# Gated cross-attention and mixture of experts on one core: memory rows picked before the branch, tokens in two buffers, later weights on ScalarE's queue, last lists after the first expert tiles

## The chip, the core and the metric

The kernel runs on one core of a Trainium2 chip. The core has TensorE for matrix products, VectorE, ScalarE and GpSimd for the rest, SyncE for issuing transfers, and 16 DMA engines that all queues share. Each engine works through its own list of instructions in order; semaphores tie the lists together. The metric is device time in microseconds (us). The kernel before takes 276.34 us, the median of 3 runs (274.91 to 276.58).

## What is computed

There are 8 sequences of 256 tokens with 512 features, and for each sequence a memory of 256 rows, of which a mask allows a part. All is float32.

```
x = x + tanh(g_x) * attention(layernorm(x), memory, mask)    # scores / sqrt(512), masked softmax, readout
y = layernorm(x)
p = softmax(y @ w_router.T)                 # 8 experts, the best 2 of each token, weights renormalised
x = x + tanh(g_f) * sum over the 2 experts of weight * (silu(y @ gate.T) * (y @ up.T)) @ down.T    # 192 inner features
```

2048 tokens with 2 experts each make 4096 pairs of a token and an expert.

## The kernel before

**Memories.** The mask leaves at most 64 rows of each memory with this data, so two memories share a tile of 128 rows, and there are four such pairs. `m_find` counts along the mask; for a pair, `m_hot` (L221) makes a matrix that marks which row goes to which place, `m_pick` (L228) multiplies it with the row numbers on TensorE, and `m_fetch` (L234) adds an offset on VectorE and has GpSimd gather the rows. Pair 0 is fetched at once. Then comes a branch (L745): the long arm treats memories with more than 64 rows and isn't taken; the short one starts the loads of the remaining tokens (L751 to 753). Pairs 1 to 3 are picked and fetched inside the loop that follows. `m_mean`, `m_centre`, `m_turn` and `m_route` centre a pair's rows, transpose them, and project them on the router. Three products on zeros (L742) stand before the branch on TensorE.

**Attention.** A written-out loop (L759) runs over 16 token tiles of 128, with the stages of different tiles interleaved: step `s` holds `a_probs` (transpose of the probabilities) and `a_values` of tile s-1, `a_scores` of tile s, `a_stats` (mean and variance on VectorE) of tile s+3, and `a_scale` (inverse deviation, GpSimd) of a later pair of tiles. The order in this loop is the order on each engine. `a_values` also yields the router's logits and the best two experts of each token.

**Lists.** Tokens are sorted into lists, one per expert, by pairs of tiles. `f_mark` counts, `f_rank` (L459) turns counts into places with three small products and VectorE, and builds two matrices of zeros and ones, `at_row` and `at_col`; four of the `at_col` products run mostly on GpSimd (L485). `f_table` (L488) adds them into one table in TensorE's accumulator. `f_weigh` (L431) computes weights on ScalarE and stores the pair's tokens with their logits as rows of `xc_d` in device memory. `read_table` turns the table into token numbers. The first tile of each expert's list uses only the first ten token tiles, so it can be gathered early; the rest needs the whole table.

**Experts.** There are 36 tiles of 128 listed tokens: 8 first tiles, 24 more, and 4 whose expert is read at run time. `gather` (L626) has GpSimd fetch a tile's rows from `xc_d` into a ring of 12 slots, which lies over the token buffer `xall`. `step(s)` (L709) does `fetch` (up to 6 tiles ahead), `gate_up` of tile s, `flip` of s-1, `turn` (transposes) of s+2 and `down` of s-2; the result is added into the output by an indirect accumulating transfer from GpSimd (L683). Steps 0 to 4 are interleaved with the end of the lists (L818 to 832): step 0 stands before the last table, steps 1 to 4 among reading it.

**Weights.** Each expert has a gate-and-up half of 768 KB and a down half of 384 KB. SyncE issues those of experts 0 to 3 in loop steps 2 to 9 and all eight halves of experts 4 to 7 at once in step 16.

Of the kernel before, what the change touches and what calls it, by code (L numbers as in the profile page):

```python
# [48 lines left out]
def gated_xattn_moe(ctx: ExitStack, tc: tile.TileContext, x, xT, ctxn, ctxT, mask, maskT, g_x, g_f, wr, wgu, wd, out):  # L49
# [62 lines left out]
    nc.sync.dma_start(out=mk8, in_=maskT)  # L112
    xall = xp.tile([P, NT, D], FP, name="xall")
    xs = [xall[:, i, :] for i in range(NT)]
    xTs = []

    def load_x(lo, hi):
        nc.sync.dma_start(out=xall[:, lo:hi, :], in_=x[lo * P:hi * P, :].rearrange("(i p) d -> p i d", p=P))

# [19 lines left out]
    def load_half(n):  # L139
        e, part = divmod(n, 2)  # L140
        if part == 0:
            nc.sync.dma_start(out=wgu_sb[:, e * GU:(e + 1) * GU], in_=wgu[:, e * GU:(e + 1) * GU])
        else:
            nc.sync.dma_start(out=wd_sb[:, e * DN:(e + 1) * DN], in_=wd[:, e * DN:(e + 1) * DN])

# [82 lines left out]
    def m_pick(p):  # L228
        n, oh = P if p else 1, KEEP.pop(("oh", p))
        for c in range(MC):  # L230
            nc.tensor.matmul(pidx[:, p:p + n], lhsT=oh[:, c].rearrange("p h v -> p (h v)"), rhs=mval[:, c, 0:n],
                             start=(c == 0), stop=(c == MC - 1))
# [63 lines left out]
    def m_hide(b):  # L296
        nc.gpsimd.tensor_scalar(hide[:, b, :], slot, cnt[:, b:b + 1], BIG, ALU.is_ge, ALU.mult)

    def long_way():
# [6 lines left out]
        mv, rs, vg, nmx, den, ng = (one[k] for k in ("l_mv", "l_rs", "l_vg", "l_nmx", "l_den", "l_ng"))  # L306
        load_x(TT, NT)
        for b in range(B):
# [43 lines left out]
    def a_stats(i):  # L352
        if i % 2 == 0:
            KEEP["mv", i // 2] = sm_.tile([P, 2, 2], FP, tag="mvp", bufs=3, name=f"mvp_{i}")
        st = sm_.tile([P, 6], FP, tag="st", name=f"st_{i}")
        nc.vector.bn_stats(st, xs[i])
        nc.vector.bn_aggr(KEEP["mv", i // 2][:, i % 2, :], st)
# [101 lines left out]
    def f_rank(k):  # L459
# [22 lines left out]
        for n in range(4):  # L482
            i = 2 * k + n // 2
            by = nc.vector if k >= NT // 2 - 2 and n < 2 else nc.gpsimd
            by.tensor_scalar(at_col[:, n, :], cols_w if by is nc.vector else cols, low[:, n:n + 1], idt[:, i, n % 2:n % 2 + 1], ALU.is_equal, ALU.mult)  # L485
# [129 lines left out]
    def x_store(k):  # L615

        nc.sync.dma_start(out=out[2 * k * P:2 * (k + 1) * P, :].rearrange("(i p) d -> p i d", p=P), in_=xall[:, 2 * k:2 * k + 2, :])

# [4 lines left out]

    KEEP["ring"], RING = 0, 12

    def gather(q):  # L626

        k = RING if apart else KEEP["ring"]
        g = xall.rearrange("p i d -> p (i d)")[:, k * XW:(k + 1) * XW]
        if not apart:  # L630
            KEEP["ring"] = (k + 1) % RING
        src = xc_d[0:EARLY * P, :] if q < E else xc_d[:, :]
        nc.gpsimd.indirect_dma_start(out=g, out_offset=None, in_=src,  # L633
                                     in_offset=bass.IndirectOffsetOnAxis(ap=gids[:, q:q + 1], axis=0))
        KEEP["xg", q] = g
# [62 lines left out]
    def at(f, s):  # L698
        if 0 <= s < len(order):
            f(order[s])  # L700

    KEEP["next"], KEEP["known"] = 0, E - 2

    def fetch(upto):
        while KEEP["next"] <= min(upto, KEEP["known"]):
            gather(order[KEEP["next"]])
            KEEP["next"] += 1

    def step(s):  # L709
        fetch(s + AHEAD)  # L710
        at(gate_up, s)
        at(flip, s - 1)
        at(turn, s + 2)
        at(down, s - 2)
# [11 lines left out]
    with tc.manual_schedule(engines={PE, DVE, ACT, POOL, SP}):  # L726
# [8 lines left out]
        a_stats(0)  # L735
        a_stats(1)
        a_scale(0)
        r_centre()
        m_hide(0)
        idle = bank([P, D], "idle")  # L740
        for n in range(3):
            nc.tensor.matmul(idle, lhsT=ones, rhs=busy, start=True, stop=True)  # L742
# [16 lines left out]
        for s in range(NT + 2):  # L759
            odd = s % 2  # L760
            p, part = divmod(s, 4)
            on(a_probs, s - 1)
            if s == EARLY + 2:
                f_close()
            on(f_centre, s - 2)
            if s:
                on(a_stats, s + 3)
                if not odd:
                    on(a_scale, (s + 2) // 2, NT // 2)
            if s != 1:  # L770
                on(a_scores, s)
            if s == 0:
                m_hot(1)
                m_hot(2)
                for b in range(1, B):
                    m_hide(b)
                more_constants()
                a_scores(1)
                m_route(0)
                m_pick(1)  # L780
                a_stats(2)
                m_fetch(1)
                a_stats(3)
                a_scale(1)
            if 1 <= s < NP - 1:
                m_pick(s + 1)
                m_fetch(s + 1)
                if s + 2 < NP:
                    m_hot(s + 2)
            if part == (2 if p else 3) and p + 1 < NP:  # L790
                m_centre(p + 1)
            on(f_square, s - 2)
            if odd:
                on(f_rank, (s - 3) // 2, NT // 2)
            if s == EARLY + 3:
                read_table(pick[:, 0:E], 0, E)
            on(a_values, s - 1)
            if s == NT:
                turn(order[0])
            if s == 1:  # L800
                nc.tensor.matmul(table, lhsT=ones[0:1, :], rhs=zero[:, 0:P], start=True, stop=True)
            if odd:
                on(f_weigh, (s - 5) // 2, NT // 2 - 1)
            else:
                on(f_scale, (s - 4) // 2, NT // 2 - 1)
                on(f_mark, (s - 2) // 2, NT // 2 - 1)
                on(f_table, (s - 4) // 2, NT // 2 - 1)
            if s == NT - 4:
# [9 lines left out]
            if s == NT + 1:  # L818
                turn(order[1])
                f_weigh(NT // 2 - 1)  # L820
                step(0)
                f_table(NT // 2 - 1)
                take_table("all")
                step(1)
                read_table(pick[:, E:NS], E, NS)
                KEEP["known"] = len(order) - 1
                step(2)
                f_total(NT // 2 - 1)
                step(3)
                numbers()  # L830
                step(4)
                read_table(sel, NS, NQ)
            if part == (1 if p else 2) and p + 1 < NP:
                m_mean(p + 1)
            if part == 3 and p + 1 < NP:
                m_turn(p + 1)
            if part == 0 and 0 < p < NP:
# [3 lines left out]
            if not odd and 3 <= (s + 4) // 2 < B:  # L841
                load_batch((s + 4) // 2)
            if 2 <= s < 2 + E:
                load_half(s - 2)
            if s == NT:
                for n in range(E, 2 * E):
                    load_half(n)
            if NT - 2 <= s <= NT:
                fetch(2 * (s - NT + 2) + 1)
        for n in range(5, len(order) + 2):  # L850
            step(n)
# [32 lines left out]
```

## Time and profile before

The profiled execution took 274.26 us.

| | |
|---|---|
| median of the runs | 276.34 us (274.91 to 276.58) |
| profiled execution | 274.26 us, its span 272.5 us |
| TensorE busy in the span | 242.0 us (89%) |
| GpSimd, VectorE, ScalarE busy | 155.7, 110.9, 109.7 us |
| gate and up products, all tiles | 99.2 us |
| down products, all tiles | 67.6 us |
| data moved | 48.20 MB, 177 GB/s on average |
| share of the 16 DMA engines by queue | 42.0% GpSimd's, 23.1% SyncE's, 4.6% ScalarE's |

In the profile PE is TensorE's products, PEld its loads of the stationary side, DVE VectorE, ACT ScalarE, POOL GpSimd and SP SyncE; L653 is line 653 of the kernel. A float32 product is recorded as two passes. A wait is put down to the event that came last in the profile. PEclk is the clock that the throttle granted, 1.00 being full speed; it shows a change only from its first event on.

### The profile page before, as it was taken

Reading aid. Unit: us, or ns where it says so; the run is one execution under the profiler, and the core shown is the slowest. Engines: PE = TensorE matmul, PEld = TensorE weight load, DVE = VectorE, ACT = ScalarE, POOL = GpSimd, SP = SyncE. Lnnn points to the kernel's source line nnn. Section 1 sums busy time; section 2 is a strip of 40 time slices with the busy share of each in tenths; the row PEclk is TensorE's granted clock in tenths of the full one; section 3 lists DMA queues with packets and bytes.
Section 4 is the critical chain, followed back from the end, with each engine's and each line's share of the span. In section 5 each row is a group of like instructions: output and inputs, shape, how many; then the busy total and the mean of one; then the engine's idle time right before and its main releaser. Section 6 shows DMA issues by size and latency. Waiting matters only on the chain.

```text
span 272.5 us, 3465 instructions
## 1 busy us (share of the span) xinstructions
PE 242.0 (89%) x1002; PEld 148.4 (54%) x1002; DVE 110.9 (41%) x447; ACT 109.7 (40%) x264; POOL 155.7 (57%) x249
## 2 busy tenths in 40 slices
PE   4788597878956999999999999999999999999950
PEld 4286374656633655556555555565555555655520
DVE  2357779897883434312312213123122131231310
ACT  1244467777775232333333323333333233333230
POOL 3898478789888006345536564584563657243360
PEclk9979899999999999999999999999999999999995
DMA  4599969999389997544565958485684595626374
GB/s 109 199 290 392 309 200 331 325 368 355 151 259 329 402 361 157 120 84 82 91 113 115 171 90 161 82 142 111 106 160 95 109 177 92 115 40 79 38 97 65
DMA packets 18684, 48.20 MB, mean 177 GB/s; under 512 B 2528, under 2 KB 2528, under 8 KB 18656
## 3 DMA queue, kind: packets, MB, share of 16 engines
q0 software_dynamic: 8416, 21.11, 42.0%
q1 hardware_dynamic: 8064, 22.04, 23.1%
q10 hardware_dynamic: 2176, 4.72, 4.6%
q8 instruction: 12, 0.20, 0.3%
q14 instruction: 16, 0.13, 0.2%
HBM read 29.51 MB, written 18.35 MB: 176 GB/s over the span
## 4 chain that ended last, share of the span: by engine, by line
PE 61%; POOL 3%; issue 2%; ACT 0%; POOLq 0%
PE pgu L653 32%; PE py L677 21%; PE pt_g L190 5%; PE pht L668 3%; POOL out L683 2%; POOL ac L485 1%; POOL spacer L503 0%; POOL xr L427 0%; ACT y L682 0%; POOLq L717 0%; PE pid L606 0%; PE table L492 0%; PE total L456 0%; POOLq L683 0%; PE total L455 0%
## 5 line engine op out<-in xcount | busy, mean ns | idle before, releaser
L653 PE MATMUL pgu<-wgu_sb,xT_g 128*128 128x384 f32 (+1 forms) x288 | 99.2, 487 | 0.0
L683 POOL DMA_INDIRECT out<-y,ids x36 | 57.1, 1586 | 69.3 <-DMA out<-y,ids 23.3
L653 PEld LDWEIGHTS pgu<-wgu_sb,xT_g 128*128 128x128 f32 x288 | 54.2, 190 | 44.4 <-issue 15.6
L677 PE MATMUL py<-wd_sb,hT 96*128 96x512 f32 (+1 forms) x144 | 67.6, 592 | 0.0
L659 DVE SCALAR_TENSOR_TENSOR th<-th,pgu 128x192 f32<-128x192 f32 x36 | 12.8, 354 | 123.4 <-ACT th L658 119.7
L633 POOL DMA_INDIRECT xall<-xc_d,gids x36 | 35.8, 995 | 23.6 <-DVE nti L589 13.6
L658 ACT ACTIVATE th<-pgu,xall 128x192 f32<-128x192 f32 x36 | 15.1, 420 | 68.0 <-PE pgu L653 63.7
L682 ACT ACTIVATE y<-py,w 128x512 f32<-128x512 f32 x36 | 24.7, 687 | 40.0 <-PE py L677 34.0
L677 PEld LDWEIGHTS py<-wd_sb,hT 96*128 96x128 f32 x144 | 24.5, 190 | 17.8 <-issue 17.5
L485 POOL TENSOR_SCALAR ac<-cols,low,idt 128x128 f16<-128x128 f32 x28 | 24.3, 877 | 8.1 <-DVE low L475 8.0
L192 ACT COPY xT_g<-pt_g 128x512 f32<-128x512 f32 x36 | 21.0, 584 | 9.8 <-PE pt_g L190 8.5
L372 PE MATMUL psc<-cT,xT 128*128 128x137 f32 x128 | 20.5, 310 | 2.8 <-ACT cT L284 2.1
L190 PE MATMUL pt_g<-ident,xall 128*128 128x128 f32 x144 | 21.6, 273 | 0.7 <-PE rank L463 0.7
L372 PEld LDWEIGHTS psc<-cT,xT 128*128 128x128 f32 x128 | 18.7, 217 | 4.4 <-ACT cT L284 3.0
L190 PEld LDWEIGHTS pt_g<-ident,xall 128*128 128x128 f32 x144 | 16.9, 140 | 1.7 <-PE rank L463 0.9
L402 PE MATMUL pav<-cn,prT 128*128 128x512 f32 x32 | 16.4, 594 | 0.0
L668 PEld LDWEIGHTS pht<-ident,h 128*96 128x96 f32 x72 | 9.1, 126 | 12.0 <-issue 7.2
L661 DVE SCALAR_TENSOR_TENSOR h<-th,xall,pgu 128x192 f32<-128x192 f32 x36 | 14.9, 415 | 1.3
L503 POOL MEMSET spacer<- 1x1 f32 x25 | 15.3, 612 | 0.0
L670 DVE COPY hT<-pht 96x256 f32<-96x256 f32 x36 | 14.9, 414 | 0.4 <-PE pht L668 0.4
L668 PE MATMUL pht<-ident,h 128*96 128x128 f32 x72 | 13.7, 273 | 0.0
L412 ACT ACTIVATE xr<-xall,xr 128x512 f32<-128x512 f32 x16 | 11.6, 723 | 2.0 <-DVE xall L408 1.9
(187 smaller groups left out, 243.1 us busy)
## 6 DMA issues: line engine op xcount, KB each, us to landing
wgu_sb<-wgu SPq DMA_DIRECT2D x8, 768.0 KB
xc_d<-xr ACTq DMA_DIRECT2D x8, 576.0 KB, 5.9
xT<-xT SPq DMA_DIRECT2D x8, 512.0 KB, 4.1
out<-xall SPq DMA_DIRECT2D x8, 512.0 KB
wd_sb<-wd SPq DMA_DIRECT2D x8, 384.0 KB, 9.0
xall<-x SPq DMA_DIRECT2D x1, 2048.0 KB
xall<-x SPq DMA_DIRECT2D x2, 512.0 KB
xall<-x SPq DMA_DIRECT2D x1, 1024.0 KB, 8.2
```

Source lines behind the costliest of these rows:

```text
L190: nc.tensor.transpose(pt[:, c, :], src[:, c * P:(c + 1) * P], ident)
L192: nc.scalar.copy(dst, pt)
L372: nc.tensor.matmul(both, lhsT=xTs[b][:, c, t * P:(t + 1) * P], rhs=cTs[p % 2][:, c, :], start=(c == 0), stop=(c == HC - 1))
L402: nc.tensor.matmul(pav, lhsT=prT, rhs=cns[p], start=True, stop=True)
L485: by.tensor_scalar(at_col[:, n, :], cols_w if by is nc.vector else cols, low[:, n:n + 1], idt[:, i, n % 2:n % 2 + 1], ALU.is_equal, ALU.mult)
L503: nc.gpsimd.memset(spacer, 0.0)
L633: nc.gpsimd.indirect_dma_start(out=g, out_offset=None, in_=src, in_offset=bass.IndirectOffsetOnAxis(ap=gids[:, q:q + 1], axis=0))
L653: nc.tensor.matmul(pgu, lhsT=xgT[:, c, :], rhs=span(wgu_sb, v * GU + c * 2 * I, 2 * I), start=(c == 0), stop=(c == HC - 1))
L668: nc.tensor.transpose(pht[:, k, :], h[:, k * IH:(k + 1) * IH], ident)
L677: nc.tensor.matmul(py, lhsT=hT[:, k, :], rhs=span(wd_sb, v * DN + k * D, D), start=(k == 0), stop=(k == 1))
L682: nc.scalar.activation(y, py, AF.Copy, scale=w)
L683: inst = nc.gpsimd.indirect_dma_start(out=out[:, :], out_offset=bass.IndirectOffsetOnAxis(ap=ids[:, q:q + 1], axis=0), in_=y, in_offset=No ...
```

## The change

- Pairs 1 to 3 of the memories are marked, picked and fetched before the branch, each with a product on one column of row numbers instead of 128. Two products on zeros stay there instead of three.
- The tokens lie in two buffers of 8 tiles; the gather ring has 14 slots, 7 over each.
- In the attention loop scores are issued for tile s+1 in step s, statistics for s+4; means, transposes and centring of the memories stand at other steps.
- Weights of experts 0 to 3 start in steps 4 to 7 and 10 to 13 on SyncE; those of experts 4 to 7 start on ScalarE's queue, one half in each of the expert steps 0 to 7.
- The first two `turn`s stand ahead of tile 15's values and logits or right behind them, the first gathers one loop step earlier. The table of pair 6 and the ranks of pair 7 stand behind step 0, the table of pair 7 behind step 1, and every later piece one step later, up to step 5. The weights of pairs 5 and 6 are made later. For the last two pairs all `at_col` products run on VectorE.

```diff
-    xall = xp.tile([P, NT, D], FP, name="xall")
-    xs = [xall[:, i, :] for i in range(NT)]
+    xhs = [xp.tile([P, NT // 2, D], FP, name=f"xh_{k}") for k in range(2)]
+    xs = [xhs[i // (NT // 2)][:, i % (NT // 2), :] for i in range(NT)]
...
     def load_half(n):
         e, part = divmod(n, 2)
+        by = nc.sync if n < E else nc.scalar
...
     def m_pick(p):
-        n, oh = P if p else 1, KEEP.pop(("oh", p))
+        n, oh = 1, KEEP.pop(("oh", p))
...
-            by = nc.vector if k >= NT // 2 - 2 and n < 2 else nc.gpsimd
+            by = nc.vector if k >= NT // 2 - 2 else nc.gpsimd
...
-    KEEP["ring"], RING = 0, 12
+    KEEP["ring"], RING = 0, 14
...
+    LOADS = (4, 5, 6, 7, 10, 11, 12, 13)
...
     def step(s):
         fetch(s + AHEAD)
+        if s < E:
+            load_half(E + s)
...
         a_stats(1)
+        m_hot(1)
+        m_hot(2)
         a_scale(0)
         r_centre()
         m_hide(0)
+        m_pick(1)
+        m_pick(2)
+        m_hot(3)
+        m_fetch(1)
+        m_fetch(2)
+        m_pick(3)
+        m_fetch(3)
         idle = bank([P, D], "idle")
-        for n in range(3):
+        for n in range(2):
...
             on(a_probs, s - 1)
+            if s == NT:
+                f_weigh((s - 6) // 2)
             if s == EARLY + 2:
                 f_close()
+            if s == NT:
+                turn(order[0])
+            if s == NT + 1:
+                turn(order[1])
             on(f_centre, s - 2)
             if s:
-                on(a_stats, s + 3)
-                if not odd:
-                    on(a_scale, (s + 2) // 2, NT // 2)
-            if s != 1:
-                on(a_scores, s)
+                if s == 1:
+                    a_stats(4)
+                on(a_stats, s + 4)
+                if odd:
+                    on(a_scale, (s + 3) // 2, NT // 2)
+            on(a_scores, s + 1 if s else 0, NT)
...
-                on(f_rank, (s - 3) // 2, NT // 2)
+                on(f_rank, (s - 3) // 2, NT // 2 - 1)
...
             if s == NT + 1:
-                turn(order[1])
+                f_weigh(NT // 2 - 2)
+                step(0)
+                f_table(NT // 2 - 2)
+                f_rank(NT // 2 - 1)
+                step(1)
                 f_weigh(NT // 2 - 1)
-                step(0)
                 f_table(NT // 2 - 1)
                 take_table("all")
-                step(1)
+                step(2)
                 read_table(pick[:, E:NS], E, NS)
                 KEEP["known"] = len(order) - 1
-                step(2)
+                step(3)
                 f_total(NT // 2 - 1)
-                step(3)
+                step(4)
                 numbers()
-                step(4)
+                step(5)
                 read_table(sel, NS, NQ)
...
-            if 2 <= s < 2 + E:
-                load_half(s - 2)
-            if s == NT:
-                for n in range(E, 2 * E):
-                    load_half(n)
-            if NT - 2 <= s <= NT:
-                fetch(2 * (s - NT + 2) + 1)
+            if s in LOADS:
+                load_half(LOADS.index(s))
+            if NT - 3 <= s <= NT:
+                fetch(2 * (s - NT + 3) + 1)
```

## What I predicted, before the result

> **What bounds the kernel now.** I read the chain of work that ended last first, then busy time by stretch, then VectorE's waits and the timelines before the experts.
>
> The chain, where the experts begin; start, length (us) and work:
>
> ```profile
> 85.54 0.81 POOL ac L485
> 86.34 0.00 issue
> 86.34 0.79 POOL ac L485
> 87.14 0.04 issue
> 87.18 0.22 PE table L492
> 87.39 2.70 PE pgu L653 x8
> ...
> 90.89 2.67 PE pgu L653 x8
> ```
>
> From 87.4 on the chain is TensorE without a hole, 4.96 us a tile (2.58 gate and up, 0.22 flip, 0.44 turn, 1.72 down). So whatever brings the third tile's gate product (90.89) forward brings the end forward by as much, unless something new starves TensorE. Before 87.4 the links are GpSimd's. Busy time by stretch:
>
> ```profile
> core 0: us, PE busy (x) PEld busy (x) DVE busy (x) ACT busy (x) POOL busy (x), PEclk, DMA share, GB/s
> ...
> 28.00:35.40 7.40, 4.36 (x18) 3.19 (x17) 5.49 (x24) 3.04 (x8) 4.40 (x7) 0.77 0.92 276
> ...
> 42.00:50.00 8.00, 6.24 (x40) 4.51 (x40) 7.06 (x33) 5.93 (x19) 6.77 (x14) 1.00 1.00 340
> ...
> 81.30:87.30 6.00, 3.65 (x19) 2.21 (x17) 1.47 (x7) 3.58 (x14) 5.25 (x7) 1.00 0.96 328
> ```
>
> In attention VectorE is fullest (7.06 of 8), GpSimd next, and TensorE is not full. Two places are hollow: 28 to 35, and 81 to 87 with VectorE at 1.47 of 6. From the waits, 35 to 81 us (total, times, longest):
>
> ```profile
> DVE sc L376 <- PE psc L372: 4.3, 5, 1.6
> ```
>
> So VectorE waits for little there but the scores. And from four engines' timelines (in brackets the idle time before, and what ended it):
>
> ```profile
> 6.47 5.03 PE L742 MATMUL idle<-busy,ones 128*128 128x512 f32 x6
> ...
> 11.46 0.19 ACT L750 COPY xall<-cn 128x1 f32<-128x1 f32 x1 [4.39 <-DMA cn<-ctxn,gid]
> ...
> 20.91 1.14 POOL L236 DMA_INDIRECT cn<-ctxn,gid  x1 [0.18 <-issue]
> ...
> 28.03 0.69 DVE L182 BATCH_NORM_STATS2 st_c<-cn 128x6 f32<-128x512 f32 x1 [2.03 <-DMA cn<-ctxn,gid]
> ...
> 31.17 0.94 PE L283 MATMUL pt_c<-ident,cc 128*128 128x128 f32 x4 [2.57 <-ACT cc L276]
> ...
> 86.39 0.22 PE L492 MATMUL table<-ac,ar 128*128 128x128 f16 x1 [1.79 <-POOL ac L485]
> ```
>
> Memory pair 1's rows, fetched at 20.9, come at 28.0, and TensorE then waits for their transposes. From 84.6 to 87.2 it waits 2.4 us for the last list, with tile 0's gate product done.
>
> **The head (rows picked ahead, one dummy product fewer).** VectorE ends its first statistics at 8.75 and makes two hot rows (0.42 each). TensorE, done with the router's sum at 6.65, does three picks from about 9.2. The first pick took 0.84 (5.20 to 6.04): they end at 11.8. Two dummies at 1.68 (5.03/3) end at 15.1; before, three ended at 11.5. The first transposes, 13.09 before, move to 15.3: +2.2. VectorE, with the third hot row and three index sums, reaches the branch at 12 instead of 9.1; its 3.64 us of idling there then end near 15.7, before it has scores. The first masked maximum came 3.70 after the transposes (16.79-13.09): now 19.0, the second 1.4 later, 20.4.
>
> The Trainium skill ("TensorE: Matmul & The Clock Gate", Part 1: The HAM clock gate) says that about 3.4 us of sustained work ends the half clock. By that one dummy fewer might leave the scores slow, or the picks wake the array. Here 6.3 us of nearly gapless products (5.2 to 11.5) left the last dummy at 0.84 a pass, against 0.43 for the same width later (L402), and the first scores at half the granted clock. So I charge nothing for the clock; by the rule the two dummies would take 1.7 and the head would be 1.6 shorter.
>
> **A new wait.** In the short arm of the branch GpSimd waits for every gather in flight: before only memory pair 0, now all four. Queued behind it are seven masks (3.95), pair 1's inverse deviation (0.95) and the constants (4.1); VectorE's third maximum waits for the first two. The three fetches issue one after another from 11.9, about 1.15 each, to 15.4. Landing: pair 0's took 3.5 after its issue ended (7.9 to 11.4), pair 1's 5.9 under a full DMA (22.05 to 28.0). The skill ("DMA: Bandwidth & Descriptors", Anatomy of one DMA) gives 2.0 us plus bytes over 436 GB/s, for 262 KB an estimate of 2.6: GpSimd goes on at 18.0. By the rows it is 18.9 to 21.3. Token loads fill the DMA from 15.7, nearer the second row; I take 20.4. The masks then start at 20.6 and the deviation is there at 25.5. VectorE's own work (five statistics of 0.8 after 20.4) would allow 24.9. So the third maximum comes at 25.6, against 23.84.
>
> **To tile 6.** From there to tile 2's update VectorE has 8.7 of work: 34.3 against 32.6. The 2.03 for pair 1's rows and the 1.60 before the maximum at 35.1 are gone, since the rows landed long before. Tile 3's update: 37.0 (36.8 before); tile 4's 4.8 on (pair statistics, ranks), tile 5's 2.6, tile 6's 4.1: 48.5 (48.5). The head's loss is repaid, with one tile's maximum (0.35) and statistics (0.8) in hand.
>
> **From there to the last pair.** Before, 28.55 from 48.5 to tile 14's logits (77.05). Of that 2.56 were waits for scores (0.46, 0.49, 1.30 and small ones), which scores issued a tile ahead remove; 1.15 is in hand. Two more list products on VectorE (L485) add 0.53. GpSimd allows it: its loop per pair was products 3.52, deviation 0.95, weights 1.15, marks 0.5 and some 1.2 through TensorE and VectorE, 7.3; the deviation now lies beside those 1.2, so 6.4, under VectorE's 6.8. With 0.4 for new small waits: 48.5+28.55-2.56-1.15+0.53+0.4 = 74.3.
>
> **The hand-over**, two chains to the third gate product.
> VectorE and ScalarE: 74.3; tiles 14 and 15 with the marks 3.5 (77.8); centre and square of tile 15 1.6; weights of pair 6 1.3; load issue 0.35; tanh 0.42; two products 0.76 (82.2); pair 7's ranks 0.9, two small ones 0.2, row matrix 0.62, four products 1.06 (85.0); table 0.3: 85.3.
> TensorE: the first ten tiles' rows are complete when pair 4's store lands, 3.8 after issue (70.55 to 74.4), now about 71.2; two gathers to 73.6, landing 4.0 later (76.85 to 80.85): 77.6; second turn, gate 0, turn, table, ranks, gate 1, flip, turn: 84.8.
> I take 85.5, against 90.89. In place of the 2.4 us wait stands one near 2, for VectorE behind gate 1 instead of GpSimd behind gate 0: the last list is still what is late. The first gathers now stand ahead of pair 5's weights on GpSimd, and pairs 5 and 6 store later; their stores are read by gather 7 alone.
>
> **Weights by ScalarE.** Eight issues of 0.35 to 0.65, where ScalarE idles about 2 us before each tanh: nothing; without that cover 4. Tightest is expert 6's gate half: begun about 0.8 into step 4, needed 9.1 later at step 6. The hardware queue took 23.1% of 272.5 for 22.04 MB, so 2.25 of all engines for 0.79 MB; steady gathers and scatters take 0.65 of 4.96, 3.2. With 1.7 of load a step on average that makes 4.9 of 4.96: full, but at half share the load lands in 4.5+2 = 6.5. The other end: pair 6's row store, issued at 83.14, let the last load go at 96.4; 13.3 would stall TensorE by 4.2. I take no stall: that store shared with a burst of larger rows, which is what the change spreads out. For the same reason it may gain: pair 7's store seems to have held gather 7 until 102.
>
> Two buffers cost nothing: the same bytes, over tiles stored long before. Fourteen slots for a lookahead of six never wait. With the lists behind steps 1 to 5, gather 7 starts near 92.4, behind scatter 0, and lands by 99; its turn is at 102.9. Past that slack of 4, TensorE waits one for one.
>
> **The sum.** 85.5-90.89 = -5.4. Profiled: span 272.5 and 1.76 around it, 274.26; after, 268.9. The runs' median is 276.34, 0.8% above that execution; from it, 270.9.
>
> **The rivals.**
> *Little head loss* (0.08): the gathers land at 18.0 and no small waits come: 1.5 to 3 less, about 268.
> *The gain goes to weights or pace* (0.19): expert 6's half lands after 13.3: 4.2 back, 275.1; for it, the full DMA; against it, that half a share suffices. Or the pairs stay at 7.3, held by some other wait: 2.6 back, 273.5.
> *Slower: the branch wait* (0.12). If the three gathers land one after another, 5.9 each from 13.0, the last lands at 30.7, 10.3 past my value, and everything behind GpSimd shifts: 281.2. Break-even is a landing at 25.8; 1% slower, 28.5. For it: 5.9 under load, and 4 MB of loads beside. Against it: the gathers of 75 to 81, 1.3 apart, landed some 4 after issue, overlapping.
> The forecast has 0.61; its own range is 268 to 274 (landing 18.9 to 22, hand-over 2 either way).
>
> Range 265.5 to 278: below, the first rival with a warm array (1.6); above, weights and pace together, short of the branch rival. Faster by over 1% (about what a measurement of this kernel can tell from no change) 0.68, within 1% 0.19, slower 0.13.
>
> **What would show it.** Right: dummies end near 15; masks begin near 20.6 behind a DMA wait; none for pair 1's rows; under 1 us of VectorE waits for scores from 42 to 70; the third gate product near 85.5 and no hole after it. Wrong: masks after 25; TensorE waiting for weights in steps 4 to 6, or for gathers at step 5; pairs still at 7.3.

## The result and the profile after

The changed kernel is slower: 279.3 us as the median of 12 runs (277.98 to 280.24) against 275.27 for the kernel before (12 runs, 272.24 to 276.8). The ratio is 1.016, with an interval of 1.013 to 1.020. Forecast were 270.9 us and a 0.68 chance of a gain.

The profiled executions say the same: span 275.9 us and time 277.98, against 272.5 and 274.26. Nearly all of the 3.4 us is there when the experts reach their third tile. First the end of the chain of waits of the changed kernel: start, length (us), work.

```profile
93.32 0.22 PE table L495
...
94.00 0.22 PE table L495
94.21 2.70 PE pgu L656 x8
```

The third gate product starts at 94.21 instead of 90.89. Behind it TensorE runs without a hole, as before, and needs as long as before (181.7 us to the end in both). So the loss lies ahead of it. TensorE's timeline there, with the idle time before an instruction and what ended it in brackets:

```profile
76.16 0.27 PE L392 MATMUL ppt<-ident,pr 128*128 128x128 f32 x1
82.03 1.09 PE L192 MATMUL pt_g<-ident,xh 128*128 128x128 f32 x4 [5.59 <-DMA xh<-xc_d,gids]
82.91 0.63 PE L403 MATMUL ppt<-cw,prT 128*128 128x128 f32 x2
83.33 1.92 PE L405 MATMUL pav<-cn,prT 128*128 128x512 f32 x2
85.04 0.99 PE L192 MATMUL pt_g<-ident,xh 128*128 128x128 f32 x4
85.86 2.75 PE L656 MATMUL pgu<-wgu_sb,xT_g 128*128 128x384 f32 x8
...
93.32 0.89 PE L495 MATMUL table<-ac,ar 128*128 128x128 f16 x4 [0.47 <-DVE ac L488]
```

The wait for the last list, 2.4 us before, has shrunk to 0.47. In its place TensorE stands 5.59 us for the first gathered tile, whose turn is now queued ahead of tile 15's routing and values (L403, L405). The values then run at half speed (1.92 instead of 1.02). Why the gather is late shows in GpSimd's timeline and in the DMA's issues between 66 and 80 us (size of each, median us to landing):

```profile
78.38 1.15 POOL L636 DMA_INDIRECT xh<-xc_d,gids  x1 [4.80 <-DMA out<-xh]
```

```profile
out<-xh SPq DMA_DIRECT2D x2, 512.0 KB, 5.6
wgu_sb<-wgu SPq DMA_DIRECT2D x1, 768.0 KB, 7.8
xc_d<-xr ACTq DMA_DIRECT2D x1, 576.0 KB
wd_sb<-wd SPq DMA_DIRECT2D x1, 384.0 KB, 8.0
```

Pair 4's row store was issued at 71.48, and GpSimd can issue the first gather only at 78.38, 6.9 us later; before it was 3.9 (70.55 to 74.42). The page names the output store (out<-xh) as the releaser, but by the trace's semaphore records that store, issued at 74.38, lands only at 78.68, behind the gather's start. The row store lands at 77.39, 5.9 us after its issue, and the gather follows 1.0 behind it, so it is the row store that it waits for. Beside it run the last of the first eight weight halves, which the change moved from steps 8 and 9 to steps 12 and 13. Busy time by stretch, the changed kernel and then the kernel before:

```profile
core 0: us, PE busy (x) PEld busy (x) DVE busy (x) ACT busy (x) POOL busy (x), PEclk, DMA share, GB/s
...
70.00:77.00 7.00, 5.13 (x28) 3.05 (x26) 6.35 (x35) 5.18 (x19) 3.50 (x4) 1.00 1.04 386
77.00:84.00 7.00, 1.97 (x7) 1.67 (x8) 2.82 (x13) 1.46 (x6) 4.72 (x7) 0.64 0.38 115
```

```profile
70.00:77.00 7.00, 5.18 (x31) 3.21 (x30) 6.29 (x36) 5.03 (x20) 5.88 (x10) 1.00 0.51 180
```

The DMA is full (1.04) where it was half idle (0.51). The head costs as well. From the timelines of VectorE, SyncE and GpSimd in the changed kernel, one fence each:

```profile
19.04 0.15 DVE L249 TENSOR_SCALAR few<-most 128x1 f32<-128x1 f32 x1 [6.59 <-DVEq L760]
...
27.14 0.28 DVE L379 CUSTOM_DVE_ANT_0 sc<-psc,hide,rs 128x64 f32<-128x64 f32 x1 [1.19 <-POOL rs L367]
```

```profile
12.94 4.35 SPq L123 DMA_DIRECT2D xT<-xT  x1
```

```profile
22.07 3.94 POOL L299 TENSOR_SCALAR hide<-slot,cnt 128x64 f32<-128x64 f32 x7 [6.73 <-remote]
```

VectorE idles 6.59 us at the branch (3.64 before), SyncE needs 4.35 for an issue that took 1.49, and GpSimd's seven masks begin at 22.07 (12.64 before), when the last of the three fetches has landed. The third masked maximum comes at 27.14 instead of 23.84. It waits 1.19 for GpSimd's deviation (`rs`), which is made behind the masks: in this execution GpSimd's wait set the end of the head, and VectorE's longer stall lay beside it.

### The profile page after: what moved, and what is told of

Same layout as the page of the kernel before. It is cut to its first block, busy times and chain, and to the rows that moved or that the text cites. A ratio compares the mean times of both kernels' runs of the same rounds, so it can differ in the third digit from the quotient of the medians.

```text
span 275.9 us, 3458 instructions
## 1 busy us (share of the span) xinstructions
PE 243.2 (88%) x1000; PEld 149.4 (54%) x1000; DVE 110.8 (40%) x451; ACT 109.8 (40%) x264; POOL 152.1 (55%) x245
## 4 chain that ended last, share of the span: by engine, by line
PE 64%; POOL 12%; DMA 7%; ACT 6%; issue 4%; DVE 3%; ACTq 1%; POOLq 0%; DVEq 0%
PE pgu L656 31%; PE py L680 21%; DMA cn<-ctxn,gid 6%; PE pt_g L192 5%; POOL ac L488 3%; PE pht L671 3%; POOL xh L636 2%; POOL out L686 2%; DMA out<-xh 1%; POOL hide L299 1%; PE pc L292 1%; ACT xr L415 1%; ACT sq L422 1%; PE psc L375 1%; ACT cn L296 1%
## 5 line engine op out<-in xcount | busy, mean ns | idle before, releaser
L656 PEld LDWEIGHTS pgu<-wgu_sb,xT_g 128*128 128x128 f32 x288 | 54.2, 190 | 43.3 <-issue 14.5
L636 POOL DMA_INDIRECT xh<-xc_d,gids x36 | 35.7, 992 | 14.6 <-issue 7.0
L661 ACT ACTIVATE th<-pgu,xh 128x192 f32<-128x192 f32 x36 | 15.1, 420 | 67.0 <-PE pgu L656 61.8
L192 PE MATMUL pt_g<-ident,xh 128*128 128x128 f32 x144 | 22.5, 280 | 5.6 <-DMA xh<-xc_d,gids 5.6
L488 POOL TENSOR_SCALAR ac<-cols,low,idt 128x128 f16<-128x128 f32 x24 | 21.0, 884 | 2.2 <-DVE low L478 2.1
L192 PEld LDWEIGHTS pt_g<-ident,xh 128*128 128x128 f32 x144 | 17.5, 145 | 7.6 <-issue 7.4
L375 PE MATMUL psc<-cT,xT 128*128 128x137 f32 x128 | 19.4, 299 | 2.5 <-POOL mvp L365 1.1
L375 PEld LDWEIGHTS psc<-cT,xT 128*128 128x128 f32 x128 | 17.7, 206 | 5.3 <-issue 2.2
L405 PE MATMUL pav<-cn,prT 128*128 128x512 f32 x32 | 17.3, 623 | 0.0
L664 DVE SCALAR_TENSOR_TENSOR h<-th,xh,pgu 128x192 f32<-128x192 f32 x36 | 14.9, 415 | 1.3
L506 POOL MEMSET spacer<- 1x1 f32 x25 | 15.3, 611 | 0.0
L415 ACT ACTIVATE xr<-xh,xr 128x512 f32<-128x512 f32 x16 | 11.6, 722 | 2.3 <-DVE xh L411 2.1
```

The lines of the kernel that those rows point to most:

```text
L192: nc.tensor.transpose(pt[:, c, :], src[:, c * P:(c + 1) * P], ident)
L375: nc.tensor.matmul(both, lhsT=xTs[b][:, c, t * P:(t + 1) * P], rhs=cTs[p % 2][:, c, :], start=(c == 0), stop=(c == HC - 1))
L405: nc.tensor.matmul(pav, lhsT=prT, rhs=cns[p], start=True, stop=True)
L506: nc.gpsimd.memset(spacer, 0.0)
L656: nc.tensor.matmul(pgu, lhsT=xgT[:, c, :], rhs=span(wgu_sb, v * GU + c * 2 * I, 2 * I), start=(c == 0), stop=(c == HC - 1))
```

## The experiments

All in one table. Ratio: to the kernel before, with its interval. Then, from the profiled execution: span, third masked maximum (the end of the head), tile 14's logits (the end of attention) and the third gate product by TensorE's timeline (0.1 to 0.2 earlier than in the chain).

| Kernel | Ratio | Span | 3rd maximum | Logits 14 | 3rd gate |
|---|---|---|---|---|---|
| before | 1 | 272.5 | 23.84 | 77.05 | 90.73 |
| changed | 1.016 (1.013-1.020) | 275.9 | 27.14 | 78.09 | 94.09 |
| e1_turns | 1.019 (1.010-1.028) | 276.1 | 27.44 | 78.40 | 94.47 |
| e2_fetch | 1.006 (1.003-1.009) | 275.3 | 25.61 | 76.77 | 92.68 |
| e3_loads | 1.010 (1.007-1.013) | 273.1 | 27.08 | 78.11 | 91.38 |
| e4_extra | 1.026 (1.016-1.036) | 278.0 | 27.30 | 80.96 | 96.20 |
| e5_both | 0.997 (0.994-1.000) | 271.8 | 25.77 | 76.74 | 89.97 |
| e6_one | 0.993 (0.990-0.996) | 270.6 | 24.05 | 75.48 | 88.52 |
| e7_sync | 1.008 (1.004-1.012) | 274.9 | 27.97 | 80.47 | 93.20 |
| e8_scalar | 0.999 (0.995-1.003) | 271.6 | 23.77 | 76.56 | 90.21 |
| e9_turns | 0.998 (0.996-1.001) | 269.2 | 23.90 | 74.70 | 87.54 |
| e10_dummy | 0.994 (0.991-0.997) | 270.6 | 24.69 | 76.52 | 88.97 |
| e11_all | 0.994 (0.992-0.997) | 270.3 | 23.93 | 76.00 | 88.45 |
| e12_order | 0.993 (0.990-0.997) | 272.1 | 25.93 | 76.20 | 88.85 |
| e13_ahead | 0.997 (0.995-0.999) | 269.6 | 23.95 | 74.95 | 88.17 |
| e14_level | 0.991 (0.989-0.994) | 270.8 | 25.45 | 74.97 | 87.65 |
| e15_level_one | 0.985 (0.979-0.990) | 269.6 | 25.73 | 73.71 | 88.02 |

A single execution's head moves by up to 2 us with the first scores' rate (below), so a profile's times are compared for their steps, and kernels by the ratios.

### The late gather: loads or order (e3_loads, e1_turns)

```diff
-    LOADS = (4, 5, 6, 7, 10, 11, 12, 13)
+    LOADS = (2, 3, 4, 5, 6, 7, 8, 9)
```

> The changed kernel with the first eight weight halves loaded in steps 2 to 9, as in the kernel before, in place of steps 4 to 7 and 10 to 13. Theory S (the last two halves, begun in steps 12 and 13, share the DMA with pair 4's row store, which is why it landed 6.9 us after issue against 3.8): the store lands about 4 us after issue, the first gather is issued near 75.6 instead of 78.38, TensorE's wait for it shrinks from 5.6 to about 2.8, the third gate product comes near 91.6 instead of 94.21: 2.6 us less, ratio to the changed kernel 0.991. Rival (the store is late because of the output stores on SyncE's queue, or the gather waits for one of those): landing and gather within 0.5 us of the changed kernel's, no change of time.

GpSimd's timeline and the busy time by stretch, with the loads early:

```profile
75.35 1.15 POOL L636 DMA_INDIRECT xh<-xc_d,gids  x1 [1.80 <-DVE inside L567]
```

```profile
70.00:77.00 7.00, 5.10 (x28) 3.02 (x26) 6.35 (x35) 5.16 (x19) 4.85 (x6) 1.00 0.41 159
```

The DMA is at 0.41, the row store issued at 71.45 lands 2.9 later, the gather goes at 75.35, again 1.0 behind the landing (the page names VectorE, and the next output store lands only at 77.10), TensorE waits 2.79, and the third gate product comes 2.7 sooner. Tile 14's logits agree with the changed kernel's within 0.02 us. All as expected: the moved weight loads made the row store late. The output stores stayed where they were.

e1_turns puts the first two turns back behind tile 15's values, in the changed kernel:

```diff
-            if s == NT:
-                turn(order[0])
-            if s == NT + 1:
-                turn(order[1])
             on(f_centre, s - 2)
...
             on(a_values, s - 1)
+            if s == NT:
+                turn(order[0])
...
             if s == NT + 1:
+                turn(order[1])
                 f_weigh(NT // 2 - 2)
```

> The changed kernel with the first two expert tiles' turns put back behind tile 15's scores and values on TensorE. Theory H (the loss of the hand-over has two links: pair 4's row store lands late, and the turn that waits for its gather stands ahead of tile 15's work on TensorE): the 5.6 us hole at 82 stays until the gather has landed near 82, but tile 15's update comes 4 us sooner, so gate 0 starts near 84.4 instead of 85.86 and the third gate product near 92.3 instead of 94.21: about 1.9 us less, ratio to the changed kernel 0.993. Rival (only the late gather counts, the order of TensorE is covered by it): third gate product within 0.4 of 94.2, no change of time.

The rival held. Tile 15's update came 3.9 us sooner (81.37 instead of 85.29), and the list was never waited for, but both turns waited for the gathers, and the first gate product took 4.44 us instead of 2.75. Order alone gained nothing as long as the gather landed at 82.

### The head (e2_fetch)

```diff
-        m_fetch(1)
-        m_fetch(2)
         m_pick(3)
-        m_fetch(3)
...
+        for n in range(1, NP):
+            m_fetch(n)
         load_batch(2)
         m_mean(0)
```

> The changed kernel with the picks kept ahead of the scores but the three fetches of memory rows issued by GpSimd behind the branch. Theory B (the branch wait of 6.59 us and GpSimd's wait of 6.73 us come from fetches and loads in flight at the branch): VectorE's wait at the branch falls to about 4, the first masked maximum comes near 19 instead of 20.34, GpSimd's masks start by 20, the third maximum near 25 instead of 27.14, and tile 14's logits 1.3 to 1.5 us sooner than 78.09; about 1.3 us off the whole. Rival (the head's loss is TensorE's later transposes and is caught up by tile 6 anyway): third maximum earlier, tile 14's logits within 0.4 of 78.09, no change of time.

VectorE's timeline and GpSimd's:

```profile
13.95 0.29 DVE L237 TENSOR_TENSOR gid<-pidx,goff 128x1 uint32<-128x1 f32 x3 [3.47 <-DVEq L757]
...
19.63 0.28 DVE L379 CUSTOM_DVE_ANT_0 sc<-psc,hide,rs 128x64 f32<-128x64 f32 x1 [3.95 <-PE psc L375]
```

```profile
17.09 0.95 POOL L238 DMA_INDIRECT cn<-ctxn,gid  x1 [0.30 <-issue]
18.13 3.94 POOL L299 TENSOR_SCALAR hide<-slot,cnt 128x64 f32<-128x64 f32 x7
```

The wait at the branch is 3.47, near the 3.64 of the kernel before, with the index sums now behind it, and the masks begin at 18.13, behind the issue of the fetches and not behind their landing. The third maximum is 1.53 sooner, tile 14's logits 1.32, the third gate product 1.41, and the ratio falls by 0.010: theory B. The first maximum came at 19.63, not 19: in this execution it waited for scores at half rate. Without the index sums VectorE also reaches the branch sooner, at 10.69 instead of 12.94, so the run doesn't tell the fetches in flight from the later arrival as the cause of its stall.

### Do the two add up? (e5_both)

The edits of e2_fetch and e3_loads together.

> The changed kernel with the three fetches behind the branch and the first eight weight halves in steps 2 to 9, both together. Theory (the two losses are separate and add: 1.5 us in the head, 2.8 in the hand-over): third gate product near 89.9, against 91.38 with the loads alone, 92.68 with the fetches alone and 90.89 in the kernel before; some 1 us under the kernel before, ratio 0.994 to 0.998. Rival (they overlap, because behind the late gather stands the last list): third gate product at 91 or later, ratio to the kernel before 1.000 or more.

Third gate product at 89.97, ratio 0.997. Of the changed kernel's 1.016, 1.9 points are gone, and the two runs apart had shown 1.0 and 0.7. So the whole loss is these two, and they hardly overlap. What is left of the change is worth about nothing, though 5.4 us were forecast. The runs below look for the rest.

### Weights by ScalarE (e7_sync, e8_scalar)

e7_sync is e3_loads without ScalarE's loads:

```diff
-        by = nc.sync if n < E else nc.scalar
+        by = nc.sync
...
-        if s < E:
-            load_half(E + s)
...
+            if s == NT:
+                for n in range(E, 2 * E):
+                    load_half(n)
```

> The changed kernel with the first eight weight halves in steps 2 to 9, and the other eight all from SyncE in step NT as in the kernel before, none from ScalarE. Theory (loading half a tile at a time from ScalarE is worth little by itself, as the loads have slack either way): within 0.5 us of the run with the loads alone (third gate product 91.4, no hole behind it). Rival (the 6.3 MB in one burst hold the gathers for steps 2 to 6 and the row stores of pairs 5 to 7): TensorE waits for gathers after the third gate product, 1 to 3 us slower than the run with the loads alone.

e8_scalar makes the opposite edit in the kernel before.

> The kernel before with one edit: the other eight weight halves begun by ScalarE, one in each of steps 0 to 7 of the experts, in place of all of them by SyncE in step NT. Theory (no stall and no gain): third gate product near 90.9 and steady 4.96 us tiles behind it, ratio 0.998 to 1.002; gather 7 lands earlier than the 102 of the kernel before without moving TensorE. Rival (expert 6's half lands late): TensorE waits up to 4.2 us for weights in steps 4 to 7, ratio 1.01 to 1.015.

Neither moved its kernel: 1.008 against 1.010, and 0.999. From the third gate product to the end it is 181.4 to 181.8 us in all four kernels. In e8_scalar gather 7 was issued at 92.21 instead of 102.0, which TensorE never felt. (The eight halves are 4.7 MB, and not 6.3 as the first expectation has it. e7_sync's later third gate comes from its head: VectorE stood 8.39 us at the branch in that execution, and tile 2's update was 1.9 us later than in e3_loads.)

### What sets the pace of attention (e4_extra, e6_one)

e4_extra adds work on GpSimd in the changed kernel:

```diff
+        if k < NT // 2 - 2:
+            nc.gpsimd.tensor_scalar(at_col[:, 3, :], cols, low[:, 3:4], idt[:, 2 * k + 1, 1:2], ALU.is_equal, ALU.mult)
```

> The changed kernel with one of GpSimd's four list products per pair done twice for pairs 0 to 5, 0.88 us more each. Theory P (the pairs' pace of 7.2 us is now GpSimd's loop through TensorE and VectorE): each pair from 35 to 70 takes about 0.8 us longer, tile 14's logits come near 82 instead of 78.09, 4 us more at the end. Rival (VectorE alone holds the pace and GpSimd has slack of 0.8 a pair, as the prediction had it): tile 14's logits within 0.8 of 78.09.

e6_one takes work off GpSimd, on top of e5_both:

```diff
-            by = nc.vector if k >= NT // 2 - 2 else nc.gpsimd
+            by = nc.vector if k >= NT // 2 - 2 or n < 1 else nc.gpsimd
```

> The kernel of the run with both (fetches behind the branch, loads in steps 2 to 9), with one of the four list products of every pair moved from GpSimd (0.88 us each) to VectorE (0.27 each). Theory G (in pairs 1 to 5 TensorE stands at the list table until GpSimd's products are done, and VectorE behind it for ranks and scores: GpSimd's loop sets the pace of 7.2): pairs of 6.8 to 7.0, tile 14's logits 1.5 to 2 us sooner than in the run with both, and the end 1 to 2 us sooner. Rival V (VectorE's own work sets the pace): each pair 0.27 longer, tile 14's logits 1.6 us later, 1.5 us slower.

Neither theory holds as it stood. With 0.88 more on GpSimd, two pairs took 15.4 us instead of 14.5, half of the addition. With 0.88 less on GpSimd and 0.27 more on VectorE it was 14.5 in both e5_both and e6_one. GpSimd's slack is about 0.4 a pair; beyond it TensorE stands in the list table, which is queued ahead of the scores. In the profile the end came sooner because the first scores ran at full rate in this execution (first maximum at 17.86 instead of 19.70); the ratios, 0.993 and 0.997, have intervals that overlap.

### The hand-over again, and the dummies (e9_turns, e10_dummy, e11_all)

e9_turns is e6_one with e1's edit, e10_dummy is e6_one with

```diff
-        for n in range(2):
+        for n in range(1):
             nc.tensor.matmul(idle, lhsT=ones, rhs=busy, start=True, stop=True)
```

and e11_all is e6_one with both.

> The run with one product moved to VectorE (e6_one), and the first two expert tiles' turns put back behind tile 15's values on TensorE. Theory (the order of TensorE cost nothing as long as the gather landed at 82, as the run with the turns alone showed; now that it lands near 76.4, tile 15's work fills the wait of 2.75 us): gate 0 near 79 instead of 79.9, the last list no longer waited for (0.84 us), third gate product near 87.2 instead of 88.5, 1.3 us less. Rival (as in the run with the turns alone, a hole of the same length stays and the products behind it run at half rate): third gate product within 0.4 of 88.5.

> The run with one product moved to VectorE (e6_one), with one dummy product of 1.7 us in place of two ahead of the first transposes. Theory (the dummies stand in the way: memory 0's centred rows are there at 12.8, its transposes wait for the dummies until 15.2 to 15.6, and the scores run at half rate in half of the executions anyway): transposes near 13.7, the first masked maximum between 17 and 18.3, and the runs' median about 0.8 us less. Rival (the second dummy is what brings the array to full rate by the first scores): scores at half rate for 4 us in every run, first masked maximum 18 to 18.3 and the later ones slow too, no gain or up to 1 us loss.

> Both edits of the two runs beside it (turns behind tile 15's values, one dummy product) on the run with one product moved to VectorE. Theory: the gains add, 2 us less than that run, ratio to the kernel before 0.984 to 0.989. Rival: only one of them counts, 0.990 or more.

TensorE's timeline in e9_turns, and the busy time by stretch, where PEclk is the granted clock:

```profile
75.76 0.63 PE L192 MATMUL pt_g<-ident,xh 128*128 128x128 f32 x4 [1.09 <-DMA xh<-xc_d,gids]
76.91 0.66 PE L192 MATMUL pt_g<-ident,xh 128*128 128x128 f32 x4 [0.53 <-DMA xh<-xc_d,gids]
78.69 4.54 PE L656 MATMUL pgu<-wgu_sb,xT_g 128*128 128x384 f32 x8 [1.12 <-ACT xT_g L194]
```

```profile
core 0: us, PE busy (x) PEld busy (x) DVE busy (x) ACT busy (x) POOL busy (x), PEclk, DMA share, GB/s
...
76.00:78.00 2.00, 1.04 (x8) 0.57 (x6) 1.69 (x11) 1.47 (x4) 1.54 (x2) 1.00 0.53 86
78.00:80.00 2.00, 1.31 (x3) 0.82 (x4) 0.41 (x1) 1.97 (x7) 1.53 (x2) 0.85 0.85 323
80.00:82.00 2.00, 2.00 (x4) 1.00 (x3) 0.00 (x0) 0.82 (x4) 1.71 (x5) 0.50 1.00 275
```

The holes got shorter and the gate product started 1.2 us sooner, but it then took 4.54 at a granted clock of 0.5. Third gate 1.0 sooner, and the ratio no better than e6_one's (0.998 against 0.993). The gain is not shown by the runs. One dummy fewer gave 0.994, the same as e6_one: the transposes came at 13.81 as expected, and the median is 0.8 us under e6_one's, but so is that of the kernel before beside it, 1.1 us, and by the ratio nothing was gained. The two together gave 0.994, where 0.984 to 0.989 were expected. All three are misses.

### The scores a tile ahead (e12_order, e13_ahead, e14_level, e15_level_one)

```diff
-                if s == 1:
-                    a_stats(4)
-                on(a_stats, s + 4)
-                if odd:
-                    on(a_scale, (s + 3) // 2, NT // 2)
-            on(a_scores, s + 1 if s else 0, NT)
+                on(a_stats, s + 3)
+                if not odd:
+                    on(a_scale, (s + 2) // 2, NT // 2)
+            if s != 1:
+                on(a_scores, s)
```

> The run with both (e5_both: fetches behind the branch, loads in steps 2 to 9), with scores, statistics and scales put back into the order of the kernel before: scores of tile s in step s in place of one tile ahead. Theory (issuing scores a tile ahead takes no time out of attention: VectorE idles 4.1 us between tile 6's update and tile 14's logits in either order, because TensorE's scores stand behind list tables, memory routes and ranks): tile 14's logits and the end within 0.6 us of the run with both. Rival (the order ahead is worth the 2.56 us of waits for scores that the kernel before shows): tile 14's logits 2 us later, 2 us slower.

It was not slower but faster, 0.993 against 0.997, with intervals that overlap. To take out the chance of the first scores, e13_ahead is e5_both with one dummy, e14_level e12_order with one dummy, side by side on one chip; e15_level_one adds e6_one's edit to e14_level.

> The run with both (e5_both), with one dummy product in place of two; scores stay a tile ahead. It is the partner of the next run, on the same chip. Theory (the score order neither gains nor costs; the difference of 0.4% between the runs with the order ahead and the order put back was the half rate of the first scores): median within 0.8 us of the next run, and pair 6's ranks within 0.6 us of it once the difference of their first masked maxima is taken off. Rival (the order ahead costs: its long wait for scores, 1.9 us before pair 5's ranks, is 0.9 with the order put back): 1 to 1.5 us slower than the next run.

> The run with the score order put back (e12_order), with one dummy product in place of two. Theory: as the run beside it with the order ahead, within 0.8 us. Rival: 1 to 1.5 us faster than it, near 0.990 of the kernel before.

> The run beside it with the score order put back and one dummy product, with one of four list products moved from GpSimd to VectorE as well. With the order put back VectorE waits 0.5 to 0.9 us at each pair's ranks, for which GpSimd's marks are late. Theory (GpSimd's lateness is then on the path): ranks no longer waited for, 1 us faster than that run, about 0.987 of the kernel before. Rival (VectorE's added 0.27 a pair takes it back): within 0.5 us of that run.

In the profiles tile 14's logits stand at 74.95 and 74.97, and the medians are 273.22 and 272.57 us. That is the theory: the order ahead gains nothing. The ratios, 0.997 and 0.991, have intervals that just fail to meet, so a cost of about 0.5% is likely, and what it would be was not found. VectorE's idle lines from 35 to 70 us with the order ahead (e13_ahead) and put back (e14_level):

```profile
44.15 0.28 DVE L379 CUSTOM_DVE_ANT_0 sc<-psc,hide,rs 128x64 f32<-128x64 f32 x1 [0.27 <-PE rank L464]
55.72 0.23 DVE L406 SCALAR_TENSOR_TENSOR xr<-ppt,r,xw 128x9 f32<-128x9 f32 x1 [0.36 <-PE ppt L403]
...
65.85 0.28 DVE L379 CUSTOM_DVE_ANT_0 sc<-psc,hide,rs 128x64 f32<-128x64 f32 x1 [1.95 <-PE rank L464]
```

```profile
36.65 0.19 DVE L468 TENSOR_TENSOR at<-hot,rank 128x32 f32<-128x32 f32 x1 [0.83 <-PE rank L466]
43.93 0.19 DVE L468 TENSOR_TENSOR at<-hot,rank 128x32 f32<-128x32 f32 x1 [0.91 <-PE rank L466]
...
58.55 0.19 DVE L468 TENSOR_TENSOR at<-hot,rank 128x32 f32<-128x32 f32 x1 [0.46 <-PE rank L466]
65.31 0.28 DVE L379 CUSTOM_DVE_ANT_0 sc<-psc,hide,rs 128x64 f32<-128x64 f32 x1 [0.91 <-PE psc L375]
```

The waits change their names; with the ones left out here they sum to 3.6 us in both. Put back, VectorE waits at the ranks, for marks that GpSimd makes late. There e6_one's edit, worth nothing with the order ahead, pays: in e15_level_one two of these are left (0.32 and 0.55, near 64), tile 14's logits come at 73.71, and the ratio is 0.985 (0.979 to 0.990), 270.27 us as the median of 6 runs. Its interval just touches e14_level's (0.989 to 0.994), so the profile shows this step more clearly than the ratios do. Its third gate product starts 0.4 us after e14_level's, but there that product ran at half rate (4.49 us against 2.80), and the span is 1.2 us shorter. This version beats both kernels.

## Why the prediction was wrong

Between the third gate product as forecast, 85.5, and as measured, 94.21, lie 8.7 us. The head gave 1.8 of them (up to tile 6: the fetches' landing was taken too early), the way from there to logits 14 gave 2.0 (waits that were to vanish only changed their names), and the hand-over 4.9 (the row store's landing was taken from a stretch with half the DMA idle). Term by term:

- **What bounds the kernel:** right. The end followed the third gate product one for one (+3.3 there, +3.4 in the span).
- **The head, TensorE:** dummies to 15.9 instead of 15.1, transposes at 16.03 instead of 15.3. The three picks ended at 12.1, not 11.8, the last one waiting for VectorE. "I charge nothing for the clock" held in this profile (first scores 3.64 us for 16 products, 3.71 before).
- **The head, VectorE: failed, but off the path.** "its 3.64 us of idling there then end near 15.7, before it has scores" took the stall over from the kernel before as a constant. It was 6.59, from 12.94 on and not from 12. In the five profiles with the three fetches ahead of the branch (changed, e1, e3, e4, e7) it was 6.6 to 8.4, in the twelve others 3.2 to 3.6. But the third maximum didn't feel it: in all five VectorE still waits there, 1.0 to 1.6 us, for GpSimd's deviation.
- **Why the stall was longer.** The Trainium skill ("Runtime: NRT & Kernel Launch", Instruction fetch mechanics) says that a taken branch outside the present window must fetch its target by DMA. The trace fits that: it has DMA packets of the kind "instruction", without the engine that they are for. In the changed kernel two of them start at 17.02 and 17.05, 4.0 us behind VectorE's branch, and VectorE goes on 1.6 behind their end; in e5_both the last of three starts 1.0 behind the branch, and VectorE goes on 1.4 behind its end. What fills the DMA meanwhile is mostly the token loads: from 13.1 to 16.9 SyncE's packets take 93.6% of the 16 engines' time, those of the fetches 5.6%. SyncE issues them from 11.45 on and doesn't wait for VectorE, so "Token loads fill the DMA from 15.7" was wrong as well (share 1.00 from 13). Whether the fetches made the stall long, or the branch that VectorE now reaches 2.2 us later, when the loads are under way, is open.
- **The new wait: right in kind, 1.5 short; this made the head late.** Landing 21.4 instead of 20.4 (6.1 us from the last issue's end, and the row used for it said 5.9 under a full DMA), masks 22.07 instead of 20.6 (0.65 behind the landing, where 0.2 was taken), third maximum 27.14 instead of 25.6. I had both ends and took a value inside the nearest row, where the trace gave every reason for the row itself.
- **To tile 6:** its update ended 50.3, not 48.5. The head's 1.5 was simply carried on.
- **From there to the last pair: failed.** That "2.56 were waits for scores" which "scores issued a tile ahead remove" is wrong. From the end of tile 6's update to tile 14's logits it was 27.8 us (forecast 25.8, before 28.5), and VectorE idled 4.2 of it (27.81 less 23.60 busy) as against 4.1 before (28.50 less 24.38). The 0.7 gained is less work, the statistics taken earlier. Scores issued ahead still stand in TensorE's queue behind tables, routes and ranks, which wait for GpSimd and ScalarE. I had checked GpSimd's sum (6.4 under 6.8), but not the order through TensorE; e4 to e6 and e12 to e15 show that the loop passes through all three.
- **The hand-over: failed, the largest term.** "pair 4's store lands, 3.8 after issue" took 3.8 from a stretch with half the DMA idle, and overlooked that the change puts two weight halves into just that stretch, though the diff shows it (LOADS ends in 12, 13). From issue to gather it was 6.9, and 3.9 again in e3. With it failed the 85.5 and its list wait near 2: the list was late by 0.47 alone. Late was the gather: TensorE had tile 15's work queued behind it, and in the chain that leads to the last list GpSimd's other gathers and pair 6's weights stand behind it. From logits 14 to the third gate it took 16.1 instead of 11.2; with the loads mended 13.4, before 13.8. The 2.2 that e3 leaves open go with a wait of 2.79 for the gather and values at half rate behind it (1.91); no run parts them further, and the other order (e9) gained nothing that the ratios show. The half rate behind TensorE's hole was not in the sum at all.
- **Weights by ScalarE, two buffers, gather 7:** right. No stall, and no gain either (e7, e8). Expert 6's gate half landed 4.6 after its issue (6.5 forecast), and gather 7 went 8.1 behind the third gate product (6.9 forecast); TensorE waited for neither. The two buffers were not tried by themselves.
- **The rivals:** the slower one, GpSimd's branch wait, was to decide from a landing of 25.8; it landed at 21.4 and cost 1.5. The mechanism that did decide, the row store beside the moved loads, was not among the rivals. That "the pairs stay at 7.3" was one, and it came true for most of its 2.6 us, for a cause it left open.

## What to carry to other kernels

A landing time belongs to the stretch of DMA in which it was measured: before it is used again, list every transfer that the change moves into the new stretch, loads of no urgency above all. A branch lies in such a stretch too: count what is in flight when each engine reaches it, and whose landing is waited for inside it. And a wait on one engine is removed by an earlier issue only if what stands in the queue between is ready as well: follow the in-order queue of the engine that serves it, not the sum of its work.

## What the runs showed of the hardware

- The first scores ran at full rate (16 products in 2.12 us) in six of the fifteen experiments and at half (3.65 to 3.99) in nine, whatever the head: e5_both and e6_one have the same one with two dummies, 3.99 and 2.12, and e10_dummy and e11_all the same one with one, 3.71 and 2.12. The Trainium skill ("TensorE: Matmul & The Clock Gate", Part 1: The HAM clock gate) has a free-running window for this, so that the switch depends on its phase; that one head gives both rates fits that. How much of the scatter in a kernel's times comes from it, no run shows.
- The PEclk row doesn't always show it: it reads 1.00 from 18 to 20 us in e5_both, where the scores took nearly twice their time (3.99 from 17.38 on).
- A hole can cost twice. After 5.59 us without work the granted clock was 0.5 and two value products took 1.92 instead of 1.02. All eleven profiles in which TensorE waited 2.2 us or more for the first gather have slow products behind it; behind 2.03 and 2.10 (e14, e12) the values took their 1.02. In e9_turns three short holes, 2.7 us in all, were enough for a gate product of 4.54 instead of 2.75.
- SyncE's issue of one load took 3.4 to 4.6 us in the five profiles with GpSimd's fetches ahead of the branch, and 1.0 to 1.1 when the fetches came later (e2, e5, e12).
- A row store of 576 KB landed 2.9 us after its issue at a DMA share of 0.41 (e3) and 5.9 at 1.04 (changed).
